# Three bfloat16 parts without GpSimd in layer 1, a bias by TensorE and an earlier rounding in layer 2

## The chip, the cores and the metric

The kernel runs on one core of one Trainium2 chip. The metric is the device time of one execution in microseconds (us); the median of several executions is compared. PE is TensorE, DVE is VectorE, ACT is ScalarE, POOL is GpSimd, and SP issues most DMAs.

## The reference

Four layers run one after the other on `x` of 4 x 256 tokens by 256 features. Each adds a gated cross-attention and a gated feed-forward of the normalised `x`. The change lies in the feed-forwards of layers 1 and 2 and in the end of layer 2's attention:

```python
def _L1_ffn_ref(x, w1, b1, w2, b2):              # 256 -> 1024 -> 256, ternary weights
    def absmean_quant(w):
        scale = jnp.mean(jnp.abs(w))
        mask = (jnp.abs(w) >= scale * 0.7).astype(w.dtype)
        return jnp.sign(w) * mask
    w1_q = absmean_quant(w1)
    w2_q = absmean_quant(w2)
    h = jnp.einsum('bsd,fd->bsf', x, w1_q) + b1
    h = jax.nn.gelu(h, approximate=False)
    out = jnp.einsum('bsf,df->bsd', h, w2_q) + b2
    return out

def _L2_ffn_ref(x, weight, bias):                # 256 -> 256, rounded to 8 bits
    ...
    x_max = jnp.max(jnp.abs(x), axis=2, keepdims=True)
    x_scale = jnp.maximum(x_max / QMAX, 1e-12)
    x_q = jnp.clip(jnp.round(x / x_scale), QMIN, QMAX).astype(jnp.int8)
    acc = jnp.einsum('bnd,od->bno', x_q.astype(jnp.int32), w_q.astype(jnp.int32))
    y = acc.astype(jnp.float32) * x_scale.astype(jnp.float32) * w_scale[None, None, :]
    y = y + bias
    return y.astype(x.dtype)

x = x + jnp.tanh(g_ffn[1]) * _L1_ffn_ref(_layernorm(x, axis=-1), ...)
x = x + jnp.tanh(g_xattn[2]) * _L2_xattn_ref(_layernorm(x, axis=-1), ctx_512, ...)
x = x + jnp.tanh(g_ffn[2]) * _L2_ffn_ref(_layernorm(x, axis=-1), L2_ffn_weight, L2_ffn_bias)
```

## The kernel before

The 1024 tokens are eight tiles of 128 (`NT`), kept on chip in `stream`; tile t is `x[t]`. Four tiles make a group of 512 (`TPG` = 4, `NG` = 2). The program is written as one stream of operations on tiles. A tile framework adds every wait, hands out the buffers (`bufs` per tag, in the order of the program), and orders the instructions of each engine before the launch: of those that are ready by its own reckoning, the one that stands earlier in the program goes first. On the chip each engine then takes its list in order. So the place of a line in the program is a priority and not a fixed position.

Layer 1's feed-forward (`ffn1`) multiplies by ternary weights, which are exact in bfloat16. To keep float32's accuracy each left operand is split into three bfloat16 parts, and each product is three matmuls into one PSUM sum. `inputs(g)` normalises a group, transposes it on TensorE and splits it, with ScalarE copies (L1547, L1549) and VectorE subtractions (L1548, L1550); its buffer `rest` serves both halves of the features. `up(g)` makes 1024 hidden features as eight blocks f of 128, two by two (f2): six matmuls each (L1565) into a PSUM tile `mm`, of which there are four, then Gelu on ScalarE (L1572). `three_terms` splits each pair: a ScalarE cast (L1493), a GpSimd subtraction (L1494), a VectorE cast (L1495) and a VectorE subtraction (L1496). `down(g)` makes the outputs of four tiles from all parts (24 matmuls a tile, L1581), and VectorE adds the bias (L1589) and the gated result (L457). `in_turn` orders these as up(0), up(1), down(0), down(1).

`weights2` rounds layer 2's feed-forward weights, multiplies them by the gate and transposes them to `wqT`. It is called ahead of `ffn1`.

Attention of layers 2 and 3 (`attention23`) takes tile after tile through `in_flight`: in turn i, `scores(i)`, the addition of tile i - 3 (L457), `weights(i - 1)` and `attend(i - 2)`. `attend` transposes the weights (L452), copies them (L453), multiplies by the values (L965), copies the result `ctxTok` (L974, buffers of tag `xn`, six in all) and multiplies by the output weights (L977). At the head of each turn one step of `beside` is taken: the second group's queries, and in layer 2 the keys and values of layer 3.

Layer 2's feed-forward (`ffn2`) loads its bias with a GpSimd DMA (L157), multiplies it by the gate (L1629), and for each group: normalises (`layernorm` with ScalarE's L392, tag `xn`), adds the bias to the four tiles on GpSimd (L1634), takes each token's largest magnitude (L1638), scales (L1639, L1640), rounds by adding and subtracting 1.5 x 2^23 (L1643, L1644), transposes (L407), and multiplies (L1649); VectorE adds the product times the token's scale to `x` (L457). Layer 3 follows in the same manner.

Of the kernel before, what the change touches and what calls it, by code (L numbers as in the profile page):

```python
# [29 lines left out]
F32 = mybir.dt.float32  # L30
# [5 lines left out]
ALU = mybir.AluOpType  # L36
AX = mybir.AxisListType
# [45 lines left out]
def tile_flamingo(ctx: ExitStack, tc: tile.TileContext, a: dict, out: bass.AP):  # L83
# [16 lines left out]
    def region(tag, cols, name):  # L100
        return sb.tile([P, cols], F32, tag=tag, name=name, bufs=1)
# [21 lines left out]
    def small(shape, name, bufs=3):  # L123
        return sb.tile(shape, F32, tag=name, name=name, bufs=bufs)
# [276 lines left out]
    def transposed(tiles, dtype=F32):  # L401

        xT = sb.tile([P, 2, TH], dtype, tag="xT", name="xT", bufs=2)
        for c in range(2):
            ps = ps_mm()
            for i, n in enumerate(tiles):
                nc.tensor.transpose(ps[:, i * P : (i + 1) * P], n[:, c * P : (c + 1) * P], ident)  # L407
            evacuate(xT[:, c, :], ps)
        return xT
# [484 lines left out]
    def attention23(layer, gate, beside):  # L894
# [88 lines left out]
        if layer == 3:  # L983
            used("L3")

    def keyed(layer, gate):
        beside = iter(())
        if layer == 2:
            values = region("wqk", 2048, "values")
            for _ in keys_values(2, region("weff", 2048, "kbd2"), values[:, :1024]):  # L990
                pass
            beside = keys_values(3, region("wvo", 2048, "kbd3"), values[:, 1024:])
        attention23(layer, gate, beside)
        for _ in beside:
            pass
# [492 lines left out]

        return loaded[f"L1_w{k}"][:, :1024].bitcast(BF16)

    def three_terms(terms, v, rest):

        nc.scalar.copy(terms[0], v)  # L1493
        nc.gpsimd.tensor_tensor(rest, v, terms[0], ALU.subtract)  # L1494
        nc.vector.tensor_copy(terms[1], rest)  # L1495
        nc.vector.tensor_tensor(terms[2], rest, terms[1], ALU.subtract)  # L1496

    def ternary1():
# [31 lines left out]
    def ffn1(gate):  # L1530
        b2_1 = output_bias("b2_1", a["L1_b2"].partition_broadcast(P))
        w1 = ternary(1).rearrange("p (c f) -> p c f", c=2)
        w2 = ternary(2).rearrange("p (f o) -> p f o", f=8)
        hidden = big[:, HIDDEN:].bitcast(BF16).rearrange("p (g k f t) -> p g k f t", g=NG, k=3, f=8)

        def inputs(g):

            two = sb.tile([P, 2, 2, TH], BF16, tag="xT", name="xT", bufs=2)
            more = t4([P, 1024], "more")
            third = more[:, :512].bitcast(BF16).rearrange("p (c t) -> p c t", c=2)  # L1540
            xn = layernorm(g)
            for c in range(2):
                ps = ps_mm()
                for i, n in enumerate(xn):
                    nc.tensor.transpose(ps[:, i * P : (i + 1) * P], n[:, c * P : (c + 1) * P], ident)
                rest = more[:, 512:]
                nc.scalar.copy(two[:, 0, c, :], ps)  # L1547
                nc.vector.tensor_tensor(rest, ps, two[:, 0, c, :], ALU.subtract)  # L1548
                nc.scalar.copy(two[:, 1, c, :], rest)  # L1549
                nc.vector.tensor_tensor(third[:, c, :], rest, two[:, 1, c, :], ALU.subtract)  # L1550
            return two[:, 0], two[:, 1], third

        xT = [inputs(0)]

        def up(g):
            for f2 in range(4):
                if g == 0 and f2 == 2:
                    xT.append(inputs(1))
                h = t4([P, 2, TH], "h")
                for j in range(2):  # L1560
                    f = 2 * f2 + j
                    ps = ps_mm()
                    for k, term in enumerate(xT[g]):
                        for c in range(2):
                            nc.tensor.matmul(  # L1565
                                ps,
                                w1[:, c, f * P : (f + 1) * P],
                                term[:, c, :],
                                start=(k == 0 and c == 0),
                                stop=(k == 2 and c == 1),  # L1570
                            )
                    nc.scalar.activation(h[:, j, :], ps, AF.Gelu, bias=b1_1[:, f : f + 1])  # L1572
                three_terms([hidden[:, g, k, 2 * f2 : 2 * f2 + 2, :] for k in range(3)], h, h)
            return hidden[:, g]

        def down(g, terms):
            for i in range(TPG):
                ps = ps_mm()
                for f in range(8):
                    for k in range(3):  # L1580
                        nc.tensor.matmul(  # L1581
                            ps[:, :D],
                            terms[:, k, f, i * P : (i + 1) * P],
                            w2[:, f, :],
                            start=(f == 0 and k == 0),
                            stop=(f == 7 and k == 2),
                        )
                y = sb.tile([P, D], F32, tag="xn", name="y", bufs=6)
                nc.vector.tensor_tensor(y, ps[:, :D], b2_1, ALU.add)  # L1589
                gated_add(g * TPG + i, y, gate)  # L1590

        in_turn(NG, up, down)
        used("L1_w1")
        used("L1_w2")
        load_experts3(EARLY3, E3)


    def weights2(gate):

        w = loaded["L2"][:, 1536:2048].rearrange("p (c d) -> p c d", c=2)  # L1600
        ws = small([P, 2], "ws", 1)
        inv = small([P, 2], "wsi", 1)
        largest = nc.vector.tensor_reduce(ws, w, AX.X, ALU.max, apply_absolute_value=True)
        behind(largest, kept["normal"])
        nc.vector.tensor_scalar(ws, ws, 1e-8, 1.0 / 127.0, ALU.max, ALU.mult)
        nc.vector.reciprocal(inv, ws)
        wq = t4([P, 2, D], "wq")
        for c in range(2):

            q = wq[:, c, :]  # L1610
            nc.vector.tensor_scalar(q, w[:, c, :], inv[:, c : c + 1], ROUND, ALU.mult, ALU.add)
            nc.vector.tensor_scalar(q, q, ROUND, 127.0, ALU.subtract, ALU.min)
            nc.vector.tensor_scalar(q, q, -128.0, ws[:, c : c + 1], ALU.max, ALU.mult)
        nc.vector.tensor_scalar(wq, wq, gate, None, ALU.mult)
        wqT = sb.tile([P, 768], F32, tag="hits", name="wqT", bufs=1)[:, :512].rearrange("p (d o) -> p d o", d=2)
# [7 lines left out]
        return wqT  # L1623

    def ffn2(gate):
        bias_2 = output_bias("bias_2", a["L2_bias"].partition_broadcast(P))
        used("L2")
        wqT = kept.pop("weights2")
        nc.gpsimd.tensor_tensor(bias_2, bias_2, gate.to_broadcast([P, D]), ALU.mult)  # L1629
        for g in range(NG):  # L1630
            xn = layernorm(g, True)

            tiles = stream[:, g * TPG : (g + 1) * TPG, :]
            nc.gpsimd.tensor_tensor(tiles, tiles, bias_2.unsqueeze(1).to_broadcast([P, TPG, D]), ALU.add)  # L1634
            xs = small([P, TPG], "xs")
            xi = small([P, TPG], "xi")
            for i, n in enumerate(xn):
                nc.vector.tensor_reduce(xs[:, i : i + 1], n, AX.X, ALU.max, apply_absolute_value=True)  # L1638
            nc.vector.tensor_scalar(xs, xs, 1.0 / 127.0, 1e-12, ALU.mult, ALU.max)  # L1639
            nc.vector.reciprocal(xi, xs)  # L1640
            for i, n in enumerate(xn):

                nc.vector.tensor_scalar(n, n, xi[:, i : i + 1], 127.0, ALU.mult, ALU.min)  # L1643
                nc.vector.tensor_scalar(n, n, ROUND, ROUND, ALU.add, ALU.subtract)  # L1644
            xqT = transposed(xn)
            for i in range(TPG):
                ps = ps_mm()
                for d in range(2):
                    nc.tensor.matmul(  # L1649
                        ps[:, :D], xqT[:, d, i * P : (i + 1) * P], wqT[:, d, :], start=(d == 0), stop=(d == 1)  # L1650
                    )
                gated_add(g * TPG + i, ps[:, :D], xs[:, i : i + 1])

    steps = [
        attention0,
# [156 lines left out]
```

## Time and profile before

| | before |
|---|---|
| median of 3 runs | 948.43 us (945.85 to 948.74) |
| the profiled execution | 947.2 us, its span 945.4 us |
| mean granted TensorE clock | 0.959 |
| PE, DVE, ACT, POOL busy | 844.9, 514.0, 288.7, 344.5 us |
| layer 1's "up" (569.0 to 602.75) | 33.75 us, PE busy 25.26 |
| layer 1's "down" (602.75 to 624.8) | 22.05 us, PE busy 21.30 |
| layer 2's attention, matmuls of the tiles (640.0 to 689.3) | 49.30 us, PE busy 43.69 |
| layer 2's feed-forward (689.3 to 709.0) | 19.70 us, PE busy 12.62, clock 0.83 |

Times in the trace count from the start of the span. A float32 matmul shows as two instructions. A busy time counts overlapping instructions of one engine once; matmuls overlap their successors, so the distance from start to start tells more of a long row of them than one's duration does. In a line of the timeline, the bracket tells how long the engine had been idle and what it waited for.

### The profile page before, as it was taken

To read this page: it belongs to the slowest core of one execution; us is meant where nothing else is said; L and a number is where in the kernel's file an instruction comes from. 1 tells how busy PE (TensorE), PEld (TensorE's weight loads), DVE (VectorE), ACT (ScalarE), POOL (GpSimd) and SP (SyncE) were. 2 spreads that over 40 slices of the span, in tenths; PEclk is the share of its full clock that TensorE was granted. 3 is DMA by queue.
4 is the path that set the end of the run, shared out by engine and by line. 5 is a ranking of instruction groups with operands and counts; after the bars stand their busy time and mean duration, and the time that the engine had idled before them with its cause. 6 is when DMAs were issued, how large, how long until landed. Compare 5 with 4: busy or idle time off the path is not lost. (4 is left out here: it accounts for less than half of the span.)

```text
span 945.4 us, 12712 instructions
## 1 busy us (share of the span) xinstructions
PE 844.9 (89%) x4464; PEld 547.3 (58%) x4467; DVE 514.0 (54%) x1299; ACT 288.7 (31%) x561; POOL 344.5 (36%) x262
## 2 busy tenths in 40 slices
PE   5999999999999998899089997899869899999994
PEld 4544335876667875676045873665545556666662
DVE  4666457756934344573146765778777865222220
ACT  2221004433222332233013436516545531122221
POOL 0455452310066777787201232502312402144321
PEclk9999999999999998999589999989989999999997
DMA  9200228101156555654570000180000011122223
GB/s 359 93 16 22 79 65 258 52 18 32 56 158 161 125 121 128 156 86 71 117 266 1 1 1 1 42 302 2 1 23 1 1 47 58 40 47 48 38 23 66
DMA packets 38762, 75.15 MB, mean 79 GB/s; under 512 B 6240, under 2 KB 26706, under 8 KB 37322
## 3 DMA queue, kind: packets, MB, share of 16 engines
q1 hardware_dynamic: 23562, 52.01, 16.4%
q0 software_dynamic: 14496, 20.47, 12.9%
q10 hardware_dynamic: 640, 1.84, 0.5%
q8 instruction: 39, 0.64, 0.3%
q14 instruction: 25, 0.20, 0.1%
HBM read 58.73 MB, written 16.61 MB: 80 GB/s over the span
## 5 line engine op out<-in xcount | busy, mean ns | idle before, releaser
L438 POOL TENSOR_TENSOR attn<-attn,sm 128x1024 f32<-128x1024 f32 x32 | 60.8, 1901 | 197.1 <-DVE sm L437 163.9
L1247 DVE SCALAR_TENSOR_TENSOR blk<-wide,weight,blk 128x176 f32<-128x176 f32 (+1 forms) x75 | 37.0, 494 | 138.0 <-ACT blk L1246 137.9
L1274 POOL DMA_INDIRECT sums<-ring,big x55 | 87.5, 1590 | 34.9 <-issue 10.8
L422 PE MATMUL wide<-xT,big 128*128 128x512 f32 x192 | 88.3, 610 | 0.3 <-ACT big L557 0.3
L684 DVE TENSOR_TENSOR rope<-wide,big 128x512 f32<-128x512 f32 x96 | 59.6, 684 | 48.8 <-PE wide L422 47.5
L1227 PE MATMUL wide<-big,blk 128*128 x220 | 77.0, 472 | 0.1
L1186 POOL DMA_INDIRECT xs<-xd,big x55 | 55.1, 1001 | 55.8 <-DMA sums<-x 35.6
L1238 PE MATMUL wide<-big,blk 128*128 x160 | 72.2, 593 | 0.5 <-DVE blk L1199 0.5
L1246 ACT ACTIVATE blk<-wide 128x176 f32<-128x176 f32 (+1 forms) x75 | 29.4, 392 | 122.5 <-PE wide L1238 60.2
L422 PEld LDWEIGHTS wide<-xT,big 128*128 128x128 f32 x192 | 35.8, 193 | 47.6 <-issue 41.3
L657 PE MATMUL mm<-vo,attnT 128*128 128x256 f32 x256 | 58.6, 382 | 0.9 <-ACT attnT L453 0.9
L1262 PE MATMUL mm<-big,blk 88*128 x220 | 57.6, 384 | 0.5 <-ACT blk L1255 0.5
L407 PE MATMUL mm<-ident,xn 128*128 128x128 f32 x112 | 19.9, 322 | 41.5 <-DVE xn L395 35.4
L657 PEld LDWEIGHTS mm<-vo,attnT 128*128 128x128 f32 x256 | 47.4, 190 | 8.7 <-ACT attnT L453 2.9
L453 ACT COPY attnT<-mm 128x512 f32<-128x512 f32 x64 | 34.6, 589 | 54.7 <-PE mm L452 54.2
L1262 PEld LDWEIGHTS mm<-big,blk 88*128 88x128 f32 x220 | 42.0, 192 | 16.0 <-ACT blk L1255 1.4
L1227 PEld LDWEIGHTS wide<-big,blk 128*128 128x128 f32 x220 | 40.7, 196 | 13.3 <-issue 1.2
L436 DVE TENSOR_REDUCE sm<-attn 128x16 f32<-128x1024 f32 x32 | 38.8, 1213 | 16.3 <-ACT attn L430 13.7
L1186 POOL DMA_INDIRECT xs<-xd,scratch x20 | 19.5, 973 | 76.2 <-PE mm L1198 54.0
L1274 POOL DMA_INDIRECT sums<-ring,scratch x20 | 31.5, 1573 | 39.2 <-ACT ring L1273 16.8
L1238 PEld LDWEIGHTS wide<-big,blk 128*128 128x128 f32 x160 | 28.8, 190 | 28.9 <-issue 28.2
L407 PEld LDWEIGHTS mm<-ident,xn 128*128 128x128 f32 x112 | 15.1, 162 | 47.2 <-ACT rstd L383 27.6
(321 smaller groups left out, 1704.3 us busy)
## 6 DMA issues: line engine op xcount, KB each, us to landing
big<-in_L_w_gate_up SPq DMA_DIRECT2D x8, 1024.0 KB, 8.2
big<-in_L_w SPq DMA_DIRECT2D x4, 1408.0 KB, 7.9
big<-in_L_w_down SPq DMA_DIRECT2D x8, 512.0 KB, 9.3
w_L_qk<-in_L_qk SPq DMA_DIRECT2D x4, 896.0 KB, 8.7
big<-in_L_w SPq DMA_DIRECT2D x4, 704.0 KB
big<-in_L_wo SPq DMA_DIRECT2D x1, 2048.0 KB, 12.9
xd<-xn SPq DMA_DIRECT2D x16, 128.0 KB, 1.8
sums<-x SPq DMA_DIRECT2D x16, 128.0 KB, 1.8
```

Of the source, the lines that this page charges most:

```text
L407: nc.tensor.transpose(ps[:, i * P : (i + 1) * P], n[:, c * P : (c + 1) * P], ident)
L422: nc.tensor.matmul(ps, w(c), xT[:, c, :], start=(c == 0), stop=(c == 1))
L436: nc.vector.tensor_reduce(sm, e, AX.X, ALU.add)
L438: nc.gpsimd.tensor_tensor(e, e, sm.unsqueeze(2).to_broadcast([P, groups, n]), ALU.mult)
L657: nc.tensor.matmul(ps[:, :D], aT[:, s, :], vo[:, s, :], start=(s == 0), stop=(s == NP - 1))
L684: nc.vector.tensor_tensor(m[:, s, :].rearrange("q (b t) -> q b t", t=S), ps[:, s, :].rearrange("q (b t) -> q b t", t=S), table, ALU.mult,)
L1186: nc.gpsimd.indirect_dma_start(out=xs, out_offset=None, in_=self.xd, in_offset=bass.IndirectOffsetOnAxis(ap=self.gather[:, b : b + 1].bitc ...
L1227: nc.tensor.matmul(ps[:, 0, : 2 * n], st[:, c * P : (c + 1) * P], self.w[:, bass.ds(r + c * 2 * n, 2 * n)], start=False, stop=(c == 1),)
L1238: nc.tensor.matmul(ps[:, k, :n], st[:, c * P : (c + 1) * P], self.w[:, bass.ds(r + (2 * c + k) * n, n)], start=(c == 0), stop=(c == 1),)
L1247: nc.vector.scalar_tensor_tensor(s, lin, self.weight.pop(b), s, ALU.mult, ALU.mult)
L1262: nc.tensor.matmul(ps[:, :D], hT[:, j * P : (j + 1) * P], self.w[: self.chunk, bass.ds(r + j * D, D)], start=(j == 0), stop=(j == self.n - 1),
L1274: nc.gpsimd.indirect_dma_start(out=self.sums[b % len(self.sums)], out_offset=bass.IndirectOffsetOnAxis(ap=self.scatter[:, b : b + 1].bitca ...
```

## The change

In layer 1, `three_terms` does its first subtraction on VectorE, and its second cast on ScalarE for every second pair (`scalar`); `inputs(1)` stands ahead of the pair f2 = 1 and no longer of f2 = 2. In layer 2, the bias is loaded by SP in `weights2`, as one row, and multiplied by the gate on VectorE; it enters the product as a matmul of a row of ones by that row, so VectorE only adds the PSUM tile to `x`. For this the token's scale is multiplied in while rounding, and the limit to 127 goes. `rounded(g)` holds normalisation and rounding; for group 0 it is called in turn 9 of attention 2, ahead of the addition of tile 6 and of `attend(7)`.

```diff
+    def beside2(keys):
+        for i in range(NT + 3):
+            if i == NT + 1:
+                kept["rounded"] = rounded(0)
+            next(keys, None)
+            yield
...
-            beside = keys_values(3, region("wvo", 2048, "kbd3"), values[:, 1024:])
+            beside = beside2(keys_values(3, region("wvo", 2048, "kbd3"), values[:, 1024:]))
...
         nc.scalar.copy(terms[0], v)
-        nc.gpsimd.tensor_tensor(rest, v, terms[0], ALU.subtract)
-        nc.vector.tensor_copy(terms[1], rest)
+        nc.vector.tensor_tensor(rest, v, terms[0], ALU.subtract)
+        (nc.scalar.copy if scalar else nc.vector.tensor_copy)(terms[1], rest)
         nc.vector.tensor_tensor(terms[2], rest, terms[1], ALU.subtract)
...
-                if g == 0 and f2 == 2:
+                if g == 0 and f2 == 1:
                     xT.append(inputs(1))
...
-                three_terms([hidden[:, g, k, 2 * f2 : 2 * f2 + 2, :] for k in range(3)], h, h)
+                three_terms([hidden[:, g, k, 2 * f2 : 2 * f2 + 2, :] for k in range(3)], h, h, f2 % 2 == 1)
...
+        bias_2 = kept_2[:1, 512:]
+        nc.sync.dma_start(out=bias_2, in_=a["L2_bias"].partition_broadcast(1))
+        nc.vector.tensor_scalar(bias_2, bias_2, gate[:1], None, ALU.mult)
+        return wqT, bias_2
+
+    def rounded(g):
+
+        xn = layernorm(g, True)
+        xs = small([P, TPG], "xs")
+        xi = small([P, TPG], "xi")
+        for i, n in enumerate(xn):
+            nc.vector.tensor_reduce(xs[:, i : i + 1], n, AX.X, ALU.max, apply_absolute_value=True)
+        nc.vector.tensor_scalar(xs, xs, 1.0 / 127.0, 1e-12, ALU.mult, ALU.max)
+        nc.vector.reciprocal(xi, xs)
+        for i, n in enumerate(xn):
+            nc.vector.tensor_scalar(n, n, xi[:, i : i + 1], ROUND, ALU.mult, ALU.add)
+            nc.vector.tensor_scalar(n, n, ROUND, xs[:, i : i + 1], ALU.subtract, ALU.mult)
+        return xn
 
     def ffn2(gate):
-        bias_2 = output_bias("bias_2", a["L2_bias"].partition_broadcast(P))
         used("L2")
-        wqT = kept.pop("weights2")
-        nc.gpsimd.tensor_tensor(bias_2, bias_2, gate.to_broadcast([P, D]), ALU.mult)
+        wqT, bias_2 = kept.pop("weights2")
         for g in range(NG):
-            xn = layernorm(g, True)
-            tiles = stream[:, g * TPG : (g + 1) * TPG, :]
-            nc.gpsimd.tensor_tensor(tiles, tiles, bias_2.unsqueeze(1).to_broadcast([P, TPG, D]), ALU.add)
...
-            xqT = transposed(xn)
+            xqT = transposed(kept.pop("rounded") if g == 0 else rounded(g))
             for i in range(TPG):
+                t = g * TPG + i
                 ps = ps_mm()
+                nc.tensor.matmul(ps[:, :D], ones[:1], bias_2, start=True, stop=False)
                 for d in range(2):
                     nc.tensor.matmul(
-                        ps[:, :D], xqT[:, d, i * P : (i + 1) * P], wqT[:, d, :], start=(d == 0), stop=(d == 1)
+                        ps[:, :D], xqT[:, d, i * P : (i + 1) * P], wqT[:, d, :], start=False, stop=(d == 1)
                     )
-                gated_add(g * TPG + i, ps[:, :D], xs[:, i : i + 1])
+                nc.vector.tensor_tensor(x[t], ps[:, :D], x[t], ALU.add)
```

More of the change, by code (lines that the diff above doesn't have):

```diff
@@ L1489, in ternary, with three_terms @@
         return loaded[f"L1_w{k}"][:, :1024].bitcast(BF16)
-    def three_terms(terms, v, rest):
+    def three_terms(terms, v, rest, scalar):
         nc.scalar.copy(terms[0], v)
-        nc.gpsimd.tensor_tensor(rest, v, terms[0], ALU.subtract)
-        nc.vector.tensor_copy(terms[1], rest)
+        nc.vector.tensor_tensor(rest, v, terms[0], ALU.subtract)
+        (nc.scalar.copy if scalar else nc.vector.tensor_copy)(terms[1], rest)
         nc.vector.tensor_tensor(terms[2], rest, terms[1], ALU.subtract)
@@ L1614, in weights2 @@
         nc.vector.tensor_scalar(wq, wq, gate, None, ALU.mult)
-        wqT = sb.tile([P, 768], F32, tag="hits", name="wqT", bufs=1)[:, :512].rearrange("p (d o) -> p d o", d=2)
+        kept_2 = sb.tile([P, 768], F32, tag="hits", name="kept_2", bufs=1)
+        wqT = kept_2[:, :512].rearrange("p (d o) -> p d o", d=2)
         ps = ps_mm()
@@ L1622, in weights2 @@
         nc.scalar.copy(wqT.rearrange("p d o -> p (d o)"), ps)
-        return wqT
+        bias_2 = kept_2[:1, 512:]
[14 more added lines that the diff above has]
+        return xn
@@ L1625, in ffn2 @@
     def ffn2(gate):
-        bias_2 = output_bias("bias_2", a["L2_bias"].partition_broadcast(P))
         used("L2")
-        wqT = kept.pop("weights2")
-        nc.gpsimd.tensor_tensor(bias_2, bias_2, gate.to_broadcast([P, D]), ALU.mult)
+        wqT, bias_2 = kept.pop("weights2")
         for g in range(NG):
-            xn = layernorm(g, True)
-            tiles = stream[:, g * TPG : (g + 1) * TPG, :]
-            nc.gpsimd.tensor_tensor(tiles, tiles, bias_2.unsqueeze(1).to_broadcast([P, TPG, D]), ALU.add)
[L1635 to L1644, printed above, removed]
-            xqT = transposed(xn)
+            xqT = transposed(kept.pop("rounded") if g == 0 else rounded(g))
```

## The prediction

> **What bounds the kernel now.** I read the page first (busy shares and the chain), then the busy time by stretch over layers 1 to 3, then the waits of each stretch, then its timeline. The page says that TensorE (PE) is the busiest engine, so time is won where PE stands still.
>
> ```profile
> PE 844.9 (89%) x4464; PEld 547.3 (58%) x4467; DVE 514.0 (54%) x1299; ACT 288.7 (31%) x561; POOL 344.5 (36%) x262
> ```
>
> The busy time by stretch shows where. The columns are the stretch, then busy time and count for PE, PEld, DVE, ACT and POOL, the granted clock, and the DMA share. The rows are layer 1's "up" matmuls, its "down" matmuls, attention 2, and layer 2's feed-forward.
>
> ```profile
> 569.00:602.75 33.75, 25.26 (x111) 11.29 (x113) 19.25 (x25) 22.45 (x34) 11.55 (x6) 0.95 0.00 0
> 602.75:624.80 22.05, 21.30 (x193) 18.76 (x192) 21.37 (x37) 4.20 (x6) 6.73 (x3) 1.00 0.52 177
> 640.00:689.30 49.30, 43.69 (x308) 25.98 (x308) 38.25 (x67) 30.79 (x58) 15.33 (x10) 0.97 0.01 1
> 689.30:709.00 19.70, 12.62 (x50) 9.88 (x51) 16.13 (x56) 7.86 (x15) 4.69 (x2) 0.83 0.08 27
> ```
>
> The change touches the first, second and fourth rows, and the end of the third. PE has no work for 8.5 us of the first row and 7.1 us of the fourth, and in these two its clock is below 1. The waits of the first row (engine and line, what it waited for, us in total):
>
> ```profile
> DVE big L1495 <- POOL h L1494: 12.2, 3, 6.9
> ACT xT L1549 <- DVE more L1548: 5.1, 2, 3.0
> PE mm L1565 <- DVE more L1548: 4.6, 2, 3.4
> PE mm L1565 <- DVE more L1550: 1.7, 1, 1.7
> ```
>
> Read upwards, this is a queue: PE waits for a subtraction of `inputs(1)`, which stands on VectorE behind a cast (L1495) that waits for GpSimd's subtraction (L1494). VectorE's timeline shows the second half of it:
>
> ```profile
> 583.03 2.59 DVE L1495 CAST big<-h 128x1024 bf16<-128x1024 f32 x1 [6.88 <-POOL h L1494]
> 585.54 0.68 DVE L1548 TENSOR_TENSOR more<-mm,xT 128x512 f32<-128x512 f32 x1
> 587.28 0.68 DVE L1495 CAST big<-h 128x1024 bf16<-128x1024 f32 x1
> 592.59 3.03 DVE L1496 TENSOR_TENSOR big<-h,big 128x1024 bf16<-128x1024 f32 x1
> 596.86 1.22 DVE L1496 TENSOR_TENSOR big<-h,big 128x1024 bf16<-128x1024 f32 x1
> ```
>
> The same instruction takes 2.59 or 0.68 us, 3.03 or 1.22 us; the long ones run beside a GpSimd subtraction. In the fourth row PE's timeline has the gap and a slow group after it:
>
> ```profile
> 688.15 1.13 PE L977 MATMUL mm<-w_L,ctxTok 128*128 128x256 f32 x4 [0.49 <-ACT ctxTok L974]
> 693.72 1.96 PE L407 MATMUL mm<-ident,xn 128*128 128x128 f32 x8 [4.44 <-DVE xn L1644]
> 696.20 5.58 PE L1649 MATMUL mm<-wqT,xT 128*128 128x256 f32 x16 [0.52 <-ACT xT L133]
> ```
>
> PE ends attention at 689.28 and then waits 4.44 us for the first group's rounding. Group 1's 16 instructions later take 3.72 us, not 5.58.
>
> **Part 1, layer 1's bfloat16 parts.** Removed: eight GpSimd subtractions (2.13 us each, the last ending at 609.5), and their slowing of VectorE: three L1495 of 2.6 us and two L1496 of 3.03 us, 5 x 1.85 = 9 us. Added to VectorE: eight subtractions 128x1024; the row beside is L1496, spaced 1.14 us start to start, so 9.1 us. The bounds are 0.6 (the cast's spacing) and 1.9 (GpSimd's L438 form); I take 1.14, the same operation and size. Moved to ScalarE: four casts at 1.05 us (L1493), 4.2 us, which takes 4 x 0.6 = 2.4 from VectorE. So VectorE's sum falls by about 2 us and, what counts more, its 12.2 us of waiting go.
>
> What is late next is a pair f2. ScalarE has two Gelus at 0.62, a cast at 1.05 and in every second pair another, 2.8 on average; VectorE 2.6; PE 12 x 0.2135 = 2.56. The three are nearly level, with ScalarE last, and ScalarE waits in order for VectorE's subtraction in the odd pairs.
>
> `inputs(1)` goes ahead of f2 = 1, not 2. Its two transposes then take two of the four PSUM slots `mm` before Gelu has freed any. From 577.96 (first Gelu) I lay the queues out by the durations above: Gelus to 579.2, cast to 580.25, the copies of `inputs(1)` to 581.45; VectorE: subtraction, cast, subtraction of pair 0 to 583.4, then L1548 to 584.1. So f = 4, which needs that slot, starts at 584.1, after a PE gap of 2.8 us (581.3 to 584.1), f = 5 at 586.7, and f = 6 at 588.0. That is no earlier than now (the matmul after the 3.4 us wait runs at 586.27). From there nothing stands in the way, since `inputs(1)` is complete at about 588 and not at 596.2: ten more f at 1.28 end at 600.8, against 602.75. The two "down" blocks take 10.64 us each; the 0.75 us that PE waits between them for a VectorE still busy with parts until 615.2 goes too (parts end near 606). Together -2.0 - 0.75 = -2.7.
>
> Here a rule is to be weighed: does the 2.8 us gap cost clock? The row: after a PE gap of 2.73 us (to 679.28) the granted clock was 0.63 and 0.52 in the next two stretches of 2 us; after 3.45 us (to 586.27) it fell to 0.50; after the 1.68 us one (to 596.27) it stayed 1.00. The Trainium skill, "TensorE: Matmul & The Clock Gate", HAM oscillation, says instead to keep idle gaps no longer than about 3.4 us. By the rule the 2.8 us gap is free and the part is worth -2.7; by the row it costs what the earlier one did (587.8 to 590.3: 6 matmuls at 0.43, not 0.21), 1.4 us. The row is of this kernel and on the same side as the gap: **-1.3**.
>
> **Part 2, the bias on PE.** Removed: GpSimd's DMA (landing in 7.6 us), its multiplication (0.70), two additions of 2.34. Nobody on the path waits for these, but VectorE's L1639 took 1.48 us beside one and 0.16 beside none. Added: per tile one f32 matmul of one row, 256 columns. Nearest is L1649: 16 instructions in 3.72, two per matmul, so 0.22 each, 0.45 per matmul; the bounds are 0.22 (two at the 0.11 spacing of the 128-column transposes L452) and 0.45. I take 0.45: 1.8 us a group. Two of four fit in PE's wait for the copy of xT (two PSUM slots are free there); exposed 0.9 a group; without that cover 1.8. The addition (0.39, L1589) for L457 (0.48) saves 0.1 a tile on VectorE.
>
> The bias's load moves to SP's queue, a DMA of 1 KB: SP has nothing between 479.1 and 602.9, so it lands far ahead; the multiplication on VectorE waits for it and is queued in front of layer 1's statistics. Cost 0 (VectorE idles 2.1 us at 566.5 to 568.65); if the DMA came late by a landing (2 us, the small loads' row), `inputs(0)` would wait that long.
>
> **Part 3, the first group's rounding ahead of attention's last tile.** Now: PE's L977 ends 689.28, matmuls of group 0 start at 696.20 and end at 701.8. After: four normalisations on ScalarE (0.52 each, 2.08) can run after tile 6's `ctxTok` (684.4), whose buffers they share; ScalarE idles 1.71 us before tile 7's copies at 686.11, so tile 7 is late by **0.4**. VectorE's four reductions, scales and eight roundings (1.6 + 0.35 + 1.95) end near 689, while it idles 3.27 us at 682.4 to 685.6 and more later. Then transposes 1.04 and copy 0.9 at full clock, bias exposed 0.9, matmuls 3.72: group 0 ends at 689.3 + 0.4 + 1.95 + 0.9 + 3.7 = 696.3, 5.5 us sooner. Waiting behind the rounding on VectorE is tile 6's addition, whose PSUM slot tile 7's L977 reuses: up to 1.4 us more; I take none, as VectorE has gaps between the reductions.
>
> Late next is group 1, from x[7] (690.2): statistics to shift 1.5, table load partly seen 0.7, normalisations 2.1, reduction 0.4, scales 0.35, roundings 1.95, additions between them 1.2, transposes 0.55, copy 0.7 = 9.4. Its matmuls start at 699.6 (now 705.23) and end at 699.6 + 3.7 + 0.9 = 704.2 (now 708.95): **-4.7**. Attention 3's transposes follow at once, as now. The two table loads amid attention 2 (673.30 and 676.61) I leave where they are; if the square root falls behind the last exponential, up to -2.6.
>
> Sum: -1.3 - 4.7 = -6.0. The profiled execution took 947.2 us (span 945.4), so 941.2; it lies 1.2 below the median of the runs, 948.4, which makes **942.4**.
>
> **Rivals.**
> - *Both gains whole* (clock kept, table loads gone, f = 4 earlier): -2.7 - 2.6 - 5.5 = -11, 937. For it: VectorE's 12 us of waiting really go. With the forecast this is the main case, 0.60.
> - *ScalarE's casts eat part 1*, and part 3 stays: 948.4 - 4.7 + 0.7 = 944.4. For it: 2.8 us a pair is the highest of the three. 0.15.
> - *The move does not happen:* the compiler orders each queue by readiness, and puts the rounding behind tile 7 after all. Then part 3 gives nothing, the bias costs up to 1.8, part 1 gives 1.3 to 2.7: 947 to 949. For it: now the shift is ready at 679.2 and the normalisation runs at 688.0. Against: it waits there for buffers which the new order hands out sooner. 0.10.
> - *Slower: ScalarE stalls in the odd pairs.* Its cast needs VectorE's subtraction, which can stand behind the previous pair's cast and subtraction (0.6 + 1.14 + 1.14 = 2.9 us), with the next Gelus behind it. Then two pairs cost ScalarE 2 x 2.3 + 1.05 + 2.9 + 0.6 = 9.1, 4.6 a pair, PE's slots come free at that pace, and the six pairs to f = 11 take 27.3 us, not the 22.2 of now (577.96 to 602.75, less the last pair's 2.6): up to +5.1, and repeated gaps of 2 us halve the clock for about 1.5 us in two of them, +3. With part 3's -4.7 that is +3.4, 952. Part 1 loses from 3.7 us a pair (22.2 / 6), and the whole turns at 4.5 (4.7 / 6 more). 0.15.
>
> **How the numbers follow.** This kernel can be told from no change beyond about 0.3%, 2.8 us: faster is below 945.6, slower above 951.3. The main case is all faster (0.60), the second mostly (0.12 faster, 0.03 same), the third mostly same (0.03, 0.06, 0.01 slower), the last 0.14 slower and 0.01 same. Faster 0.75, same 0.10, slower 0.15. The range goes from 935 (the whole gains and a run at the low end, -2) to 949.5 (the third case's upper end); it leaves out the last case.
>
> **What would show it.** No POOL in layer 1's feed-forward; L1495's form at 0.68 and L1496's at 1.2 throughout; "up" about 31 us and not 33; PE's gap of 4.44 us behind the last L977 below 1.5; the granted clock 1 in layer 2's feed-forward; from the last L977 to the end of its matmuls 15 us and not 19.7. I am wrong if ScalarE waits over 1 us for the subtraction in odd pairs, if tile 7's L977 is late by over 2 us, or if layer 3 grows.

## The result, and the profile after

| | before | after |
|---|---|---|
| median, 20 runs each | 948.59 us (945.25 to 959.39) | 944.12 us (939.94 to 949.78) |
| the profiled execution | 947.2 us, span 945.4 | 945.55 us, span 943.7 |
| mean granted TensorE clock | 0.959 | 0.956 |

The ratio is 0.9961 [0.9946, 0.9976]: faster by 3.7 us (2.3 to 5.1). The forecast was 6.0 us. The total is near it, but its parts are not: two large misses of opposite sign nearly cancel. The busy times of the page hardly show that: PE has 8 us more, GpSimd 23 us less.

```profile
PE 853.0 (90%) x4480; PEld 551.8 (58%) x4483; DVE 509.9 (54%) x1304; ACT 292.0 (31%) x565; POOL 321.4 (34%) x250
```

The busy time by stretch of after (columns as before: PE, PEld, DVE, ACT, POOL, clock, DMA share, GB/s) has "up", "down", attention 2, and layer 2's feed-forward with the transposes for layer 3:

```profile
569.60:596.30 26.70, 23.20 (x111) 11.04 (x113) 21.15 (x30) 24.16 (x35) 0.00 (x0) 1.00 0.00 1
596.30:617.40 21.10, 21.10 (x193) 18.73 (x192) 17.12 (x36) 6.09 (x8) 0.00 (x0) 1.00 0.54 180
632.60:682.40 49.80, 43.97 (x310) 26.42 (x311) 40.97 (x79) 31.44 (x59) 15.34 (x10) 0.97 0.00 1
682.40:704.80 22.40, 19.15 (x73) 11.94 (x71) 14.25 (x50) 7.78 (x14) 0.00 (x0) 0.85 0.08 24
```

Layer 1 lost its idle time and its clock loss: "up" takes 26.7 us and no longer 33.75, at clock 1.00, with no POOL at all. Layer 2's feed-forward did not improve. PE is busy there for 19.15 us where it was 12.62 (some 1 us of it the transposes for layer 3), and the clock is still 0.85.

To compare kernels, each profile is cut at the same events of PE: "up" is from the first transposes of `inputs(0)` to the first "down" matmul; "down" to its last matmul; attention 2 to the end of its last L977; layer 2's feed-forward ("ffn 2") to the first query matmul of layer 3 (L422); attention 3 to the end of its last L977; then the rest. All in us, one profile each; what follows uses this table.

| kernel | up | down | attention 2 | ffn 2 | attention 3 | rest |
|---|---|---|---|---|---|---|
| before | 33.86 | 22.04 | 64.49 | 20.79 | 50.25 | 183.96 |
| after | 26.79 | 21.12 | 64.98 | 22.40 | 51.61 | 186.19 |
| layer1 | 26.78 | 21.13 | 64.80 | 20.62 | 50.25 | 184.68 |
| layer2 | 35.91 | 21.13 | 65.96 | 22.38 | 50.26 | 184.57 |
| nopool | 28.31 | 21.12 | 64.48 | 20.68 | 50.26 | 184.07 |
| inputs_early | 32.74 | 21.58 | 64.88 | 21.16 | 50.26 | 183.73 |
| dve_only | 26.79 | 21.12 | 65.90 | 22.37 | 53.35 | 184.99 |
| round_late | 26.79 | 21.13 | 64.84 | 23.88 | 50.27 | 186.21 |
| no_bias | 26.79 | 21.12 | 64.96 | 18.07 | 50.26 | 184.42 |
| bias_last | 26.80 | 21.12 | 64.94 | 27.34 | 55.96 | 184.40 |
| pool_bias | 26.79 | 21.12 | 64.87 | 21.14 | 50.44 | 184.72 |
| pool_warm | 27.98 | 21.13 | 65.16 | 22.27 | 53.51 | 184.56 |
| pool_split | 26.79 | 21.13 | 64.96 | 18.52 | 50.27 | 186.43 |
| split_warm | 26.78 | 21.12 | 64.95 | 18.37 | 50.27 | 187.59 |

So after has -7.07 and -0.92 in layer 1, +0.49 in attention 2, +1.61 in ffn 2, +1.36 in attention 3. The rest and what lies ahead of layer 1 scatter from profile to profile by more than 3 us, with or without an edit there. None of that is counted as an effect.

How far can one profile be trusted in the other stages? Kernels with the same code in a stage tell. Ffn 2 agrees well: 20.62 to 21.16 in before, layer1, nopool and inputs_early, and 22.37 to 22.40 in after, layer2 and dve_only. "Up" agrees less: 33.86 in before and 35.91 in layer2, 26.79 in after and 27.98 in pool_warm. Attention 3, which no edit touches, has 50.25 to 55.96. The last section says why.

The page's lines moved by 7 in layer 1 (L1501 is the subtraction that was L1494, L1572 the "up" matmul), and in layer 2 the bias matmul is L1658, the product L1660, its addition L1663, the rounding L1642 to L1647.

### The profile page after: what moved, and what is told of

Same layout as the page of the kernel before. It is cut to its first block, busy times and chain, and to the rows that moved or that the text cites. A ratio compares the mean times of both kernels' runs of the same rounds, so it can differ in the third digit from the quotient of the medians.

```text
span 943.7 us, 12733 instructions
## 1 busy us (share of the span) xinstructions
PE 853.0 (90%) x4480; PEld 551.8 (58%) x4483; DVE 509.9 (54%) x1304; ACT 292.0 (31%) x565; POOL 321.4 (34%) x250
## 3 DMA queue, kind: packets, MB, share of 16 engines
q0 software_dynamic: 14448, 20.33, 12.7%
## 4 chain that ended last, share of the span: by engine, by line
PE 37%; DVE 6%; ACT 4%; POOL 1%; issue 1%; DMA 1%; POOLq 0%; ACTq 0%; DVEq 0%
PE wide L1245 7%; PE mm L422 4%; PE mm L1269 3%; PE wide L1455 2%; PE mm L657 2%; PE mm L1588 2%; PE mm L1572 2%; PE mm L452 1%; PE wide L935 1%; PE wide L642 1%; PE mm L1476 1%; PE mm L977 1%; PE mm L407 1%; DVE sm L436 1%; POOL attn L438 1%; PE mm L1660 1%
## 5 line engine op out<-in xcount | busy, mean ns | idle before, releaser
L422 PE MATMUL wide<-xT,big 128*128 128x512 f32 x192 | 88.3, 609 | 0.3 <-ACT big L557 0.3
L422 PEld LDWEIGHTS wide<-xT,big 128*128 128x128 f32 x192 | 35.7, 193 | 47.6 <-issue 41.5
L1206 DVE COPY blk<-mm 128x256 f32<-128x256 f32 x75 | 31.3, 419 | 18.7 <-PE mm L1205 17.6
```

The costliest lines, as they stand in the source:

```text
L422: nc.tensor.matmul(ps, w(c), xT[:, c, :], start=(c == 0), stop=(c == 1))
```

## Layer 1: where the eight microseconds came from

The waits of after in its "up" stretch, the longest first, have none on POOL, and PE's longest is 1.7 us, where L1565 waited 4.6 and 1.7 before:

```profile
ACT kept L1630 <- PE mm L1627: 3.8, 1, 3.8
PEld L1572 <- issue: 3.5, 5, 1.8
DVE more L1557 <- ACT xT L1556: 3.4, 2, 3.1
...
PE mm L1572 <- ACT xT L1556: 1.7, 1, 1.7
```

The edits were taken one at a time: all of layer 1's on the kernel before (layer1), `three_terms` alone (nopool), the earlier `inputs(1)` alone (inputs_early), and the whole change without ScalarE's casts (dve_only).

```diff
 # layer1: both hunks on before; nopool: the first; inputs_early: the second
-        nc.gpsimd.tensor_tensor(rest, v, terms[0], ALU.subtract)
-        nc.vector.tensor_copy(terms[1], rest)
+        nc.vector.tensor_tensor(rest, v, terms[0], ALU.subtract)
+        (nc.scalar.copy if scalar else nc.vector.tensor_copy)(terms[1], rest)
...
-                if g == 0 and f2 == 2:
+                if g == 0 and f2 == 1:
 # dve_only: on after
-                three_terms([hidden[:, g, k, 2 * f2 : 2 * f2 + 2, :] for k in range(3)], h, h, f2 % 2 == 1)
+                three_terms([hidden[:, g, k, 2 * f2 : 2 * f2 + 2, :] for k in range(3)], h, h, False)
```

> Layer 1's edits alone (the three parts without GpSimd, inputs(1) ahead of f2 = 1) on the kernel before. Theory A, read from the changed kernel's trace: layer 1's feed-forward falls from 55.8 us to 47.8, and nothing is given back in layer 2; median 8 us below before, ratio about 0.9915, so 3 to 4 us faster than the whole change. Theory B, the prediction's own sizes: 1.3 to 2.7 us faster, ratio 0.997 to 0.9985.

> The kernel before with the three parts on VectorE and ScalarE alone; inputs(1) stays ahead of f2 = 2. Theory A (GpSimd's subtraction was the stall, the place of inputs(1) hardly matters): layer 1's up 27 to 28.5 us instead of 33.9, ratio 0.992 to 0.9935. Rival (the earlier inputs(1) brings most of it, as its third part came at 596.2): up 31 to 32, ratio 0.998.

> The kernel before with inputs(1) ahead of f2 = 1 alone; GpSimd keeps its subtraction. Theory A: up within 1.5 us of before's 33.9, ratio 0.9985 to 1.001. Rival: up 29 to 31, ratio 0.995 to 0.997.

> The changed kernel with all second casts of layer 1 on VectorE, none on ScalarE. If the share given to ScalarE matters: up 1 to 2 us longer than 26.8, or the parts end so late that down waits, and the kernel 1 to 2 us slower than the changed one (ratio 0.997 to 0.999). If it does not (TensorE sets up's pace, VectorE has slack until down(1)): up and down unchanged, 26.8 and 21.1, ratio 0.995 to 0.997.

| kernel | median (runs) | ratio to before |
|---|---|---|
| layer1 | 939.71 (8) | 0.9923 [0.9898, 0.9947] |
| nopool | 940.72 (5) | 0.9923 [0.9903, 0.9943] |
| inputs_early | 946.75 (22) | 0.9980 [0.9964, 0.9996] |
| dve_only | 946.20 (12) | 0.9972 [0.9942, 1.0001] |

Layer 1's edits alone make the kernel 7.3 us faster, more than the whole change. Most is GpSimd's subtraction leaving: nopool has -5.55 in "up" and -0.92 in "down". The earlier `inputs(1)` gives 1.1 by itself and 1.5 on top of it, which is within what "up" differs by with the same code; by its ratio inputs_early is 1.9 us faster than before (0.4 to 3.4), while layer1 and nopool have the same ratio. ScalarE's casts give nothing here: in dve_only VectorE does all of them, and "up" and "down" are 26.79 and 21.12 as in after. In its profile attention 2 and 3 are 0.9 and 1.7 us longer than in after's, with PE at half clock for a while: one L977 of each takes 2.07 and 2.01 us, where the others take 1.13.

## Layer 2: why ffn 2 became longer

Here are the opposite half (layer 2's edits on before), and after with one thing undone: the rounding of group 0 back behind attention (round_late), or no bias matmuls, so that the output lacks this bias (no_bias).

```diff
 # layer2: on after, layer 1 as in before
-        nc.vector.tensor_tensor(rest, v, terms[0], ALU.subtract)
+        nc.gpsimd.tensor_tensor(rest, v, terms[0], ALU.subtract)
...
 # round_late: on after
-                kept["rounded"] = rounded(0)
+                pass
...
-            xqT = transposed(kept.pop("rounded") if g == 0 else rounded(g))
+            xqT = transposed(rounded(g))
 # no_bias: on after
-                nc.tensor.matmul(ps[:, :D], ones[:1], bias_2, start=True, stop=False)
...
-                        ps[:, :D], xqT[:, d, i * P : (i + 1) * P], wqT[:, d, :], start=False, stop=(d == 1)
+                        ps[:, :D], xqT[:, d, i * P : (i + 1) * P], wqT[:, d, :], start=(d == 0), stop=(d == 1)
```

> Layer 2's edits alone (bias by TensorE, first group rounded ahead of tile 7, bias loaded by SP). Theory A: from the end of attention 2's last L977 to the first query matmul of attention 3 about 22.4 us instead of 20.8, attention's end 0.4 later; 1.5 to 2.5 us slower than before, ratio 1.0015 to 1.0025. Theory B: 4.7 us faster, ratio 0.995.

> The changed kernel with group 0's rounding at its old place behind attention 2 (bias still by TensorE). Theory A (group 1's statistics, rounding and transposes set the end, and group 0's early rounding only makes PE wait between the groups): about as long as the changed kernel, within 2 us; attention 2's last tile 0.4 us sooner. Theory B: 5 us longer than the changed kernel.

> The changed kernel without the eight bias matmuls: layer 2's feed-forward bias is left out of the output. Theory A (the matmuls stand between the rounding's transposes and run at half clock): layer 2's feed-forward is shorter by 3 to 5 us than in the changed kernel (22.4 to about 18.5), group 1's first product matmul comes 2 us sooner. Theory B (two of four hidden, 0.9 us exposed a group): shorter by 1.8 us. If they were hidden altogether: no difference.

| kernel | median (runs) | ratio to before |
|---|---|---|
| layer2 | 955.12 (6) | 1.0109 [1.0064, 1.0153] |
| round_late | 945.70 (14) | 0.9984 [0.9959, 1.0009] |
| no_bias | 937.61 (6) | 0.9895 [0.9865, 0.9925] |

So layer 2's edits are a loss, the bias matmuls cost 4.33 us in ffn 2 (22.40 against 18.07; the ratios of after and no_bias differ by some 6 us, give or take 3), and the earlier rounding gains only 1.48 there, less 0.14 in attention 2. (layer2's median is 7.4 us above before's on the same chip, its ratio stands for 10.3 with an interval from 6.1; its profile, the fastest of its runs, has a span only 4.8 longer, of which 3.1 fell in attention 2 and ffn 2 and 2.05 in "up", at a gap that lost the clock. The rest of its loss was not found.)

PE's timeline of after shows both. After the last L977 the transposes come at once, so the rounding did move, but then PE stands still between the groups:

```profile
681.26 1.13 PE L977 MATMUL mm<-w_L,ctxTok 128*128 128x256 f32 x4 [0.55 <-ACT ctxTok L974]
682.23 1.11 PE L407 MATMUL mm<-ident,xn 128*128 128x128 f32 x8
683.27 1.12 PE L1658 MATMUL mm<-kept,ones 1*128 1x256 f32 x4
684.33 1.99 PE L1660 MATMUL mm<-kept,xT 128*128 128x256 f32 x8
686.25 0.69 PE L1658 MATMUL mm<-kept,ones 1*128 1x256 f32 x2
...
692.46 0.63 PE L407 MATMUL mm<-ident,xn 128*128 128x128 f32 x2 [2.77 <-DVE xn L1647]
693.01 1.21 PE L1658 MATMUL mm<-kept,ones 1*128 1x256 f32 x2
694.16 0.69 PE L407 MATMUL mm<-ident,xn 128*128 128x128 f32 x2
...
695.92 1.11 PE L407 MATMUL mm<-ident,xn 128*128 128x128 f32 x4
697.29 3.02 PE L1660 MATMUL mm<-kept,xT 128*128 128x256 f32 x8 [0.25 <-ACT xT L133]
```

The gap of 2.77 us is followed by PE at half clock: the two instructions of a bias take 1.21 instead of 0.69, eight of the product 3.02 instead of 1.99. And the bias matmuls, which wait for no transpose, go between the transposes, and ScalarE's and VectorE's copies of these come later for it. The same place in no_bias, with the gap and the half clock, but no biases:

```profile
684.34 3.72 PE L1659 MATMUL mm<-kept,xT 128*128 128x256 f32 x16 [0.57 <-ACT xT L133]
691.79 2.22 PE L407 MATMUL mm<-ident,xn 128*128 128x128 f32 x8 [3.73 <-DVE xn L1647]
694.39 5.35 PE L1659 MATMUL mm<-kept,xT 128*128 128x256 f32 x16 [0.38 <-ACT xT L133]
```

The 4.33 us of the bias come apart by start times. Group 1's transposes start 10.07 us after attention's end (682.39) in after, and 8.96 in no_bias (from 682.83): 1.1, since VectorE has to do group 0's additions on its way to group 1's rounding, and these wait for longer products. From there to the products it is 4.83 against 2.60: 2.2 for two biases and the transposes among them at half clock. The products then take 6.4 against 5.35: 1.0.

Why group 1 is late is in VectorE's timeline of after, where x[7] is complete at 683.24:

```profile
685.49 0.43 DVE L1663 TENSOR_TENSOR x<-mm,x 128x256 f32<-128x256 f32 x1 [0.87 <-PE mm L1660]
685.95 0.43 DVE L380 BATCH_NORM_STATS2 st<-x 128x6 f32<-128x256 f32 x1
686.36 0.42 DVE L1663 TENSOR_TENSOR x<-mm,x 128x256 f32<-128x256 f32 x1
686.70 0.17 DVE L384 RECIPROCAL rstd<-rstd 128x4 f32<-128x4 f32 x1
...
689.73 0.43 DVE L1663 TENSOR_TENSOR x<-mm,x 128x256 f32<-128x256 f32 x1 [0.28 <-PE mm L1660]
690.07 0.73 DVE L1642 TENSOR_REDUCE xs<-xn 128x1 f32<-128x256 f32 x2
```

The square root that L384 needs was done on ScalarE at 685.46. L384 runs at 686.70, because VectorE takes its list in order, and two additions of group 0 (L1663) with statistics for layer 3 (L380) stand in front of it, the first waiting 0.87 us for PE. The last two reductions stand likewise behind an L1663 that waited 0.28. Group 0's early finish thus delays group 1. In round_late VectorE rounds both groups while PE is still at group 0, and the clock is back: PE goes from group 0's products (to 694.0) straight to group 1's transposes, and those take 0.38 for two and 0.66 for four. Its wait of 3.18 us lies ahead of group 0 instead, a loss of the same kind in another place.

## Tests of the bias's price

If the bias matmuls are dear because of where they stand, another place or engine should help. bias_last makes them the last of each sum. pool_bias gives the addition back to GpSimd, as one instruction 128x1024 a group, and pool_split as four of 128x256. pool_warm and split_warm add work for PE between the groups, to hold the clock.

```diff
 # bias_last: on after
-                nc.tensor.matmul(ps[:, :D], ones[:1], bias_2, start=True, stop=False)
                 for d in range(2):
...
+                nc.tensor.matmul(ps[:, :D], ones[:1], bias_2, start=False, stop=True)
 # pool_bias: on after, no bias matmul, the bias loaded by SP to 128 rows; in rounded(g), behind layernorm
+        nc.gpsimd.tensor_tensor(tiles, tiles, bias_2.unsqueeze(1).to_broadcast([P, TPG, D]), ALU.add)
 # pool_split: in its place
+        for t in range(g * TPG, (g + 1) * TPG):
+            nc.gpsimd.tensor_tensor(x[t], x[t], bias_2, ALU.add)
 # pool_warm: pool_bias, and ahead of group 1's transposes
+                for _ in range(24):
+                    nc.tensor.transpose(ps[:, :P], ident, ident)
 # split_warm: pool_split, and there
+                for _ in range(12):
+                    nc.tensor.matmul(ps[:, :P], ident, ident, start=True, stop=True)
```

> The changed kernel with each bias matmul after the tile's two product matmuls and not ahead of them. If what costs is the bias matmuls' place between group 1's transposes: layer 2's feed-forward 20.5 to 21.5 us, not 22.4. If it is their number (eight of 0.45 us, some at half clock): 22 to 23 us, since none is then hidden behind a wait.

> The changed kernel with its bias added to the tiles by GpSimd again, group 0's also ahead of tile 7 (loaded by SP as 128 rows, multiplied on VectorE). Theory A (the bias matmuls cost 4.3 us in layer 2's feed-forward and GpSimd's addition is hidden): layer 2's feed-forward to the first query matmul 18 to 18.6 us instead of 22.4, ratio to before 0.988 to 0.9905, below both kernels. Rival (GpSimd's additions slow VectorE's rounding, or tile 7): 20 to 21 us, ratio 0.991 to 0.993.

> GpSimd's bias addition again, but as one addition a tile, each behind its own normalisation, so that it ends before VectorE's scales (L1646, 1.49 and 1.88 us beside the one large addition, 0.15 beside none). Theory: layer 2's feed-forward 18 to 18.8 us, ratio 0.989 to 0.991, the fastest kernel with the whole output. Rival (the tile's additions still stand beside the scales or the reductions): 20 to 21.5 us, 0.993 to 0.995.

> The one before in this list with 24 transposes of the identity added on TensorE between the two groups' products, into a PSUM tile that nobody reads: 2.6 us of work in a gap of about 3.7. Theory A (the gap halves the clock of group 1's transposes and products): the granted clock stays 1 there, and layer 2's feed-forward is 2 to 3 us shorter still, 15.5 to 16.5. Rival (group 1 is held by VectorE's rounding alone, the clock being incidental): no shorter, or longer by up to 1 us.

> The one before with twelve ordinary float32 matmuls of the identity (2.6 us) between the two groups' products, into a PSUM tile that nobody reads. Transposes in that place did not keep the clock. If ordinary matmuls do: the clock stays 1 through group 1 and layer 2's feed-forward falls by 2 to 3 us. If not: the same length, or up to 1.5 us longer.

| kernel | median (runs) | ratio to before |
|---|---|---|
| bias_last | 951.88 (12) | 1.0043 [1.0020, 1.0066] |
| pool_bias | 942.38 (9) | 0.9945 [0.9928, 0.9962] |
| pool_split | 940.37 (12) | 0.9924 [0.9897, 0.9952] |
| pool_warm | 945.76 (22) | 0.9970 [0.9953, 0.9988] |
| split_warm | 942.45 (12) | 0.9940 [0.9913, 0.9968] |

bias_last is the worst, and worse than was expected of either cause: ffn 2 takes 27.34 us. What the place between the transposes costs does come back: group 1's products start 2.63 us after the first of its transposes (691.59 to 694.22), as in no_bias (2.60), and not 4.83 as in after. But then these products with their biases take 12.7 us and not 6.4. The busy time by stretch has PE nearly without a pause and its clock at 0.50 from 694 to 710. The last three of these four stretches are:

```profile
698.00:702.00 4.00, 4.00 (x10) 2.32 (x8) 1.58 (x5) 0.00 (x0) 0.00 (x0) 0.50 0.00 0
702.00:706.00 4.00, 4.00 (x9) 1.99 (x8) 1.03 (x3) 0.00 (x0) 0.00 (x0) 0.50 0.00 0
706.00:710.00 4.00, 4.00 (x12) 2.59 (x12) 1.97 (x6) 0.93 (x3) 0.00 (x0) 0.50 0.00 0
```

The half clock lasts to 711.9 and comes again from 725.6 to 732.4, which is why its attention 3 is the longest too (55.96).

pool_bias wins back 1.26 of the bias's 4.33 us in ffn 2, and pool_split 3.88. By the start times after attention's end, 1.03 of the 2.62 us between the two have come when group 0's products start and 1.11 more when group 1's transposes do; the other 0.48 lies in group 1's products, where the clock came back sooner. The 2.14 are in the main one tiny instruction. VectorE's L1646 scales 128x4 numbers; beside the long GpSimd addition it takes 1.49 us in group 0 and 1.87 in group 1. First GpSimd and VectorE of pool_bias in group 1, then of pool_split:

```profile
690.26 2.34 POOL L1641 TENSOR_TENSOR x<-x,kept 128x1024 f32<-128x1024 f32 x1 [9.14 <-ACT xn L392]
690.76 1.87 DVE L1646 TENSOR_SCALAR xs<-xs 128x4 f32<-128x4 f32 x1
```

```profile
693.20 2.77 POOL L1641 TENSOR_TENSOR x<-x,kept 128x256 f32<-128x256 f32 x4 [7.75 <-ACT xn L392]
695.17 0.15 DVE L1646 TENSOR_SCALAR xs<-xs 128x4 f32<-128x4 f32 x1
```

In both groups of pool_bias L1646 ends within 0.03 us of GpSimd's instruction (at 681.14 and 692.63), while a reciprocal that runs inside GpSimd's time, at 690.66, takes its usual 0.18. This fits what the Trainium skill ("SBUF — State Buffer", SBUF: two separate sides) describes: GpSimd and VectorE share a pair of ports by an exclusive lock, held for a whole instruction, and a VectorE instruction that needs the pair is blocked until then. Shorter GpSimd instructions hold it for less. The two L1646 of pool_bias are 3.06 us above twice 0.15; pool_split still pays some 0.9 (L1646 takes 0.46 in group 0, and L388 0.71 and not 0.15 in group 1). The 2.2 between them are near the 2.14 of the start times.

The attempts to hold the clock did not pay. In pool_warm 24 transposes fill PE from 692.05 to 694.83. After a gap of 2.84 us group 1's own eight follow at full clock, in two lots of 0.70 (pool_bias has 2.21 for the eight at half clock), but then the 16 product instructions take 6.76 us, where pool_bias has 5.34 and full clock 3.72. So the loss was put off and not avoided; the last section shows its course. With ordinary matmuls by the identity (split_warm) the gap left is 1.68 us, and the products take 4.94 where pool_split has 4.87: no gain either.

By its ratio pool_split beats before by 0.76% and lies some 3.5 us below after. It leads layer1 by 2 us in the stages, but not in the medians; the two can't be told apart (0.9924, 0.9923), and its interval just touches after's.

## Why the prediction was right in sum, and wrong in its steps

The sum was near by luck. Layer 1 gave 6.7 us more than part 1 said, and attention 2 and ffn 2 together lost 2.1 us where parts 2 and 3 had 4.7 to win.

**Part 1, predicted -1.3, measured -8.0** (-7.07 in "up", -0.92 in "down"). The mechanism was right: GpSimd was the slow member, its slowing of VectorE went (L1502 takes 0.69 and L1503 1.22), parts end at 605.0 ("near 606"), and the 0.75 for "down" was about right. The step that failed is the queue laid out by hand from the first Gelu on. It put the subtractions of `inputs(1)` behind pair 0's parts, L1548 at 584.1, and so a PE gap of 2.8 us in front of f = 4. On the chip the transposes of `inputs(1)` go between the matmuls of f = 0 while PE waits anyway, and both subtractions that free a PSUM slot (L1548, now L1555) come ahead of pair 0's first (L1501, in DVE's timeline of after):

```profile
576.75 0.69 DVE L1555 TENSOR_TENSOR more<-mm,xT 128x512 f32<-128x512 f32 x1
580.50 0.69 DVE L1557 TENSOR_TENSOR more<-more,xT 128x512 bf16<-128x512 f32 x1 [3.07 <-ACT xT L1556]
581.30 0.69 DVE L1555 TENSOR_TENSOR more<-mm,xT 128x512 f32<-128x512 f32 x1
581.91 1.22 DVE L1501 TENSOR_TENSOR h<-h,big 128x1024 f32<-128x1024 f32 x1
```

So f = 4 starts at 580.73, f = 5 at 582.04 and f = 6 at 583.34, which the prediction had at 588.0. The ten f from there take 12.95 us (12.8 predicted). The whole miss lies in that start and in the clock loss subtracted for the gap. (The queue also lets f = 5 start 2.6 us after f = 4, twice a block's 1.28, without a reason. If that is f = 4 at half clock, the loss of 1.4 us was taken off twice.) With no gap, the weighing of row against rule decided nothing: by the rule -2.7, by the row -1.3, both of a gap that did not come.

**Part 2, predicted 0.9 us a group exposed (its -4.7 includes this), measured 4.33 for both.** Two sizes failed. The matmul by itself: four biases and the products of group 0 took 6.4 us from 683.27, against 3.72 for the products, so 0.67 each and not 0.45. In a row of four instructions it is 0.53; alternating with products it also slows these. And what it delays: VectorE's additions, and at half clock the transposes of group 1, neither of which was in the sum. That hardly anything waited for GpSimd's additions was true, so there was little to gain.

**Part 3, predicted -5.5 for group 0 and -4.7 in the end; measured +1.61 in ffn 2.** With the bias on GpSimd in four pieces (pool_split) or left out (no_bias), ffn 2 is 2.27 or 2.72 us shorter than before's, so the earlier rounding and what goes with it are worth about half of the forecast at best. Group 0's products began 1.94 us after attention's end, where before it was 6.92, a gain of 5.0, and attention 2 paid 0.14 against round_late (0.4 predicted). The step that failed is the 9.4 us from x[7] to group 1's products; it took 14.05 (683.24 to 697.29). To the shift it was 4.07, not 2.2 (VectorE's list); from the normalisations to the end of the reductions 1.3, not 0.4; from the last rounding to the products 3.6, not 1.25 (clock and bias matmuls). The additions had been given 1.2 of VectorE's time, but not their waits for PE. What was wrong was less an amount of work than an order: an instruction that waits for PE was put in front of work that PE will need.

**The rivals.** ScalarE did not stall: apart from one wait of 2.91 us, at the last pair and off the path, it kept the pace of PE. The move did happen. "Both gains whole" is not what happened either, although layer 1 gave even more than it. Of the signs named, those of layer 1 came ("up" was 26.8, below the 31 given), and PE's gap of 4.44 did go; but the clock of ffn 2 stayed below 1, and from the last L977 to the end of ffn 2's matmuls it took 21.3 us and not 15.

Attention 3 grew by 1.36 us in after's profile, which the prediction named as a sign against it. The same gap before the same matmul, first in after, then in before:

```profile
750.23 1.75 PE L977 MATMUL mm<-w_L,ctxTok 128*128 128x256 f32 x4 [1.44 <-ACT ctxTok L974]
```

```profile
755.49 1.13 PE L977 MATMUL mm<-w_L,ctxTok 128*128 128x256 f32 x4 [1.45 <-ACT ctxTok L974]
```

The gap of after lies whole in one of the windows that the last section describes (747.19 to 750.60, PE busy for 1.61 us of it), and the next window is at half clock. That of before falls across two, in which PE is busy for 2.49 and 2.25 us. layer2, round_late and no_bias have 50.26 or 50.27 there, as before has, so it is not a cost of the edit as such. How often it happens in the runs without a profile is not known.

## What to carry to other kernels

Work started early is worth only what the last consumer of the shared in-order engine gains: before moving group 0 ahead, read what of group 0 then stands in front of group 1. A cheap matmul that replaces an addition on an engine that hardly anything waits for is no gain, and here half of its price, 2.2 of 4.33 us, came from its place between transposes whose copies are waited for, part of it by the half clock there. Where GpSimd works beside VectorE, several short instructions can cost less than one long one. And a stage with pauses of PE has no one length: read the clock of the same stage in several profiles before a difference of 1 or 2 us is put down to an edit.

## What the hardware showed that was not expected

- The clock is not lost at a fixed gap. In attention 2, the same L977 behind a gap of 2.73 or 2.74 us took 1.13 us (full clock) in layer2 and dve_only, 1.29 in no_bias, 1.37 in split_warm and 2.01 in pool_warm; in the first two the loss came one L977 later, behind a gap of 0.49. A gap of 1.44 cost clock in after and one of 1.45 none in before; 2.05 cost some in layer2's "up", where 1.68 cost none in before.
- It is lost by windows. In all 14 profiles each stretch of full or half clock lasts a whole multiple of 3.41 us from one change to the next, so the changes lie on a grid, and the grid lies differently in each profile. Cut on it, the busy time by stretch of after between the groups of ffn 2 (PE's is the first after the comma, the clock is the 0.50 or 1.00 behind POOL) is:

```profile
689.16:692.57 3.41, 0.64 (x4) 0.24 (x3) 3.09 (x13) 0.60 (x2) 0.00 (x0) 1.00 0.00 0
692.57:695.99 3.42, 3.42 (x9) 1.46 (x10) 1.40 (x7) 0.60 (x1) 0.00 (x0) 0.50 0.00 0
695.99:699.40 3.41, 3.16 (x10) 2.39 (x10) 0.70 (x2) 2.06 (x4) 0.00 (x0) 0.50 0.00 0
699.40:702.81 3.41, 3.41 (x13) 1.98 (x13) 2.67 (x8) 0.00 (x0) 0.00 (x0) 1.00 0.00 0
```

A window with little work is paid for in the next. Over the 14 profiles, all 80 windows at full clock in which PE was busy for less than 1.4 us were followed by half clock, and only 29 of the 3323 in which it was busy for over 2.05 us. The Trainium skill ("TensorE: Matmul & The Clock Gate", Part 1) has such a free-running window of 3413 ns; its advice to keep gaps below some 3.4 us was not enough here, since a shorter gap costs when it lies whole in one window. The prediction's row, one gap and one clock, was one draw.
- Transposes held the clock. pool_warm's first window here has no other work of PE, and the clock stays; the loss comes from the next window:

```profile
692.52:695.94 3.42, 2.31 (x22) 2.08 (x20) 3.40 (x10) 1.82 (x5) 1.82 (x1) 1.00 0.00 0
695.94:699.35 3.41, 1.32 (x8) 0.80 (x8) 2.96 (x11) 2.18 (x4) 0.53 (x1) 1.00 0.00 0
699.35:702.76 3.41, 2.85 (x8) 2.24 (x8) 1.24 (x3) 0.58 (x1) 0.00 (x0) 0.50 0.00 0
```

The Trainium skill (the same page, Part 4) says that a transpose does not count as busy for the clock gate in the way of other work; this trace shows the contrary.
- A half clock can last through unbroken work: 20.5 us in bias_last (691.4 to 711.9), most of it with two one-row instructions after every four full ones. One-row matmuls seem not to count as work for the clock. In the 14 profiles eight windows at half clock were filled by PE to over 90%, a third or more of it with one-row matmuls, and all eight were followed by half clock again. Of the 75 filled as far by transposes and by matmuls of 128 rows and over 8 columns alone, 74 were followed by full clock. Four of the eight are bias_last's, and one-row matmuls were not tried by themselves.
- An f32 matmul of one row costs no less than one of 128 rows (0.53 us in a row of four instructions, against 0.46 for a product's).
